# Biases as rows, a later wo and a new order on VectorE in a two-layer graph network on one core

## The chip, the cores and the metric

The kernel runs on one core of one Trainium2 chip. Its time is the device time of one execution in microseconds (us), and the figure of a version is the median of several runs. The engines are TensorE (PE in the profile, with PEld for its weight loads), VectorE (DVE), ScalarE (ACT), GpSimd (POOL) and SyncE (SP). SP, ACT and POOL also issue DMAs; in the profile, their issuing side is SPq, ACTq and POOLq.

## The reference

64 graphs of 256 nodes with 512 features each, float32, share one adjacency matrix of 0 and 1. Layer 0 is an attention of 8 heads masked by that matrix, layer 1 a product with it, and a layer norm follows each:

```python
q = (x @ Wq + bq).reshape(b, n, H, HD)          # H = 8, HD = 64
k = (x @ Wk + bk).reshape(b, n, H, HD)
v = (x @ Wv + bv).reshape(b, n, H, HD)
scores = einsum('bqhd,bkhd->bhqk', q, k) / sqrt(HD) + (1 - adj) * -1e9
out = einsum('bhqk,bkhd->bqhd', softmax(scores), v).reshape(b, n, d)
x = layernorm(x + out @ Wo + bo)
x = layernorm(x + einsum('nm,bmd->bnd', adj, x) @ weight + bias)
```

## The kernel before

**Tiling.** The graphs are taken in 32 pairs. The features of a pair lie transposed, 128 features by 512 columns (two graphs of 256 nodes), four such tiles to a pair. Each product of a pair with a 512 by 512 matrix is made in blocks of 128 output rows by 512 columns, in one PSUM bank each, by `product` (line 335 does all its matmuls). [...] a matrix is split into three parts (high, low and diff): ScalarE makes the high part, VectorE the low part and the difference, ScalarE scales one of them. So an ordinary block takes three times four matmuls. Only the first two blocks of queries and keys of pair 0 multiply unsplit float32, since nothing is split yet.

**Order.** The order on each engine is the order of the calls, written out by hand: TensorE, VectorE, ScalarE and GpSimd are under a manual schedule. `start()` is the beginning, `first(w)` and `second(w)` are one pair's steady state, `ending()` the end. `do(...)` runs its arguments one after the other. What is split in the first pairs is also written to scratch memory in DRAM by GpSimd (`keep`, line 135) and read back for each later pair (`load_w`, line 113).

**Queues.** SP issues its DMAs in the order of the code: four blocks of 128 rows of x for pair 0 (tiles `low`, line 177), columns of Wk, Wq and Wk (`load_columns`, line 172), the biases bq and bk by `by_partition` (line 90), the other halves of Wq and Wk, the adjacency, Wv (line 194) and x of pair 1 (line 81). ACT issues one, the first 128 columns of Wq. GpSimd issues four small loads of bv in `small_ones` (line 202), and the four loads of Wo in `load_o` (line 213).

**The stage of the change.** `x_first(i)` transposes block i of x on TensorE against the identity `ident` (line 262: four transposes of 128 by 128 into one bank), and VectorE (i even, line 268) or ScalarE (i odd, line 266) copies the bank to SBUF in two halves. `x_high` and `x_rest` split these tiles (lines 281, 285, 286). Then come the blocks of the first product: `(block, "q", 0, 0)`, `k 0`, `q 1`, `k 1`. ScalarE evacuates each with its bias as a column of 128 values (line 369). Between them the weights are split (`ring_high` line 121, `ring_rest` lines 126 and 127, `ring_scale` line 130), `x_t` transposes x of the next pair on VectorE (line 273), and `adj_t` transposes the adjacency on TensorE (lines 229 and 230). `scores` (line 451) and the masks (line 472) follow. `test_adj` (lines 234 to 236) checks the adjacency's values on VectorE.

The columns of biases are in `numbers`, a tile of 128 by 32: columns 0 to 3 for bq, 4 to 7 for bk, 8 to 11 for bv. bv has another order of its elements, because heads are interleaved in the transposed output; it enters only through `bv_wo` (line 242), which multiplies it with Wo, and `with_bv` (lines 249 and 250), which adds that row to bo.

Of the kernel before, what the change touches and what calls it, by code (L numbers as in the profile page):

```python
# [8 lines left out]
F32 = mybir.dt.float32  # L9
# [6 lines left out]
P = 128  # L16
# [19 lines left out]
def fast(tc, x, adj, wq, bq, wk, bk, wv, bv, wo, bo, w1, b1, out):  # L36
# [6 lines left out]
    nc = tc.nc  # L43
    B, N, D = x.shape
    HD = D // H
    DC = D // P
    NC = N // P
    NP = B // 2
    HF = D // 2
# [11 lines left out]
    one = pool("one", 1)  # L61
    two = pool("two", 2)
# [5 lines left out]
    banks = pool("banks", 8, space=bass.MemoryType.PSUM)  # L68

    XC, XF, XP, R, Q, K, V, E, SM, O, SET, HL, ST, LN = ({} for _ in range(14))  # L70
    RAW, SCRATCH, W, UNCUT, BEGUN = {}, {}, {}, {}, {}
# [14 lines left out]
            nc.sync.dma_start(t, xr[p])  # L86
            R[p] = [t[:, b] for b in range(2)]

    def by_partition(b, t):
        nc.sync.dma_start(t, b.rearrange("(c p) -> p c", p=P))  # L90

    def on_all(b, name):
        t = cpool.tile([P, D], F32, name=name)
        nc.sync.dma_start(t, b.partition_broadcast(P))
        return t
# [74 lines left out]
    def load_columns(queue, which, a, b):  # L170
        w = wq if which == "q" else wk
        queue.dma_start(RAW[which][:, :, a:b], w.rearrange("(c p) e -> p c e", p=P)[:, :, a:b])

    load_columns(nc.scalar, "q", 0, P)
    for i in range(4):
        t = four.tile([P, D], F32, name="low")
        nc.sync.dma_start(t, xc[0, i // 2, i % 2])  # L177
        rows0.append(t)
    for which, c in ("k", 0), ("q", P), ("k", P):
        load_columns(nc.sync, which, c, c + P)  # L180
    ident = one.tile([P, P], F32, name="z")
    numbers = cpool.tile([P, 32], F32, name="numbers")
    nc.scalar.activation(numbers[:, 16:17], ones[:, 0:1], AF.Exp)
    bq_s, bk_s, bv_s = (numbers[:, i * DC:(i + 1) * DC] for i in range(3))
    power, first_of_32 = numbers[:, 12:14], numbers[:, 14:15]
    by_partition(bq, bq_s)
    by_partition(bk, bk_s)
    for which in "qk":
        load_columns(nc.sync, which, HF, D)
    adj_s = two.tile([P, NC, N], F32, name="vc")  # L190
# [7 lines left out]

    def small_ones():

        for d in range(DC):
            nc.gpsimd.dma_start(bv_s[:, d:d + 1], bv.rearrange("(g h a i u) -> g a h i u", h=4, a=2, i=32, u=1)[d // 2, d % 2])
        nc.gpsimd.memset(power, -0.5)
        nc.gpsimd.memset(first_of_32, 0.0)
        for d in range(DC):
            nc.gpsimd.memset(first_of_32[d * 32:d * 32 + 1], 1.0)

    def load_o():
        for k in range(DC):
            if k % 2 == 0:  # L210
                raw_o = two.tile([P, 2, D], F32, name="hl")
            RAW["o", k] = raw_o[:, k % 2]
            nc.gpsimd.dma_start(RAW["o", k], wo[k // 2 * HF:(k // 2 + 1) * HF].rearrange("(h a i) e -> a h i e", h=4, a=2)[k % 2])

    def load_l():
        t = two.tile([P, DC, D], F32, name="r")
# [37 lines left out]
    def x_first(i):  # L254
        if i == 0:
            for h in range(2):
                XF[0, "both", h] = one.tile([P, 2, D], F32, name=f"e{2 + h}")
                for d in range(2):
                    XF[0, 2 * h + d] = XF[0, "both", h][:, d]
        pt = banks.tile([P, DC, P], F32, name="ps")  # L260
        for d in range(DC):
            nc.tensor.transpose(pt[:, d, :], rows0[i][:, d * P:(d + 1) * P], ident)  # L262
        for h in range(2):
            to, of = XF[0, "both", h][:, :, i * P:(i + 1) * P], pt[:, 2 * h:2 * h + 2]
            if i % 2:
                nc.scalar.activation(to, of, AF.Copy)
            else:
                nc.vector.tensor_copy(to, of)

    def x_t(p, k):  # L270
        if p < NP:
            XF[p, k] = two.tile([P, D], F32, name="xT")
            nc.vector.transpose(XF[p, k], XC.pop((p, k)))
            if p > 1 or k > 1:
                load_x(p + k // 2, (k + 2) % DC)
# [162 lines left out]
    def scores(p, g, between=[]):  # L438
        if not 0 <= p < NP:
            return  # L440
        for b in range(2):
            for kc in range(NC):

                sc = [banks.tile([P, 2, N], F32, name="ps") for s in range(2)]
                keys = slice(b * N + kc * P, b * N + (kc + 1) * P)
                for a in range(2):
                    digits = (1, 0, 2) if (p, g) != (0, 0) else (0,)
                    for i in digits:
                        for s in range(2):
                            r = slice(s * HD, (s + 1) * HD)  # L450
                            nc.tensor.matmul(sc[s][:, a, :], K[p, g][r, a, i, keys], Q[p, g][r, a, i, b * N:(b + 1) * N],  # L451
                                             start=i == digits[0], stop=i == digits[-1])
                if (p, g) == (NP - 1, 1):

                    names = (("x", two), ("high", four), ("low", four), ("diff", four))
                    name, pool_of = names[2 * b + kc]
                    e = [pool_of.tile([P, 2, N], F32, name=name) for _ in range(2)]
                    whole = []
                else:
                    e = one.tile([P, 2, 2, N], F32, name=f"e{2 * b + kc}")  # L460
                    whole, e = [e.rearrange("p s a n -> p (s a) n")], [e[:, s] for s in range(2)]
                E[p, g, b, kc] = e, whole
                if (b, kc) == (1, 1):
                    do(*between)
                for s in range(2):
                    nc.scalar.activation(e[s], sc[s], AF.Exp, scale=(RHO if (p, g) != (0, 0) else 1.0) * qscale)  # L466
# [15 lines left out]
    def masks(p, g, b):  # L482
        return [(masked, p, g, b, 0), (masked, p, g, b, 1), *([(summed, p, g, b)] if (p, g) != (NP - 1, 1) else [])]
# [145 lines left out]
    def do(*tasks):  # L629
        for t in tasks:  # L630
            for f, *args in (t if isinstance(t, list) else [t]):
                f(*args)
# [54 lines left out]
    def steps_of(*args):  # L687

        h, r, s = ([(f, *args, k) for k in range(4)] for f in (ring_high, ring_rest, ring_scale))
        return h[:2], r[:1] + h[2:3] + r[1:2] + h[3:], r[2:3] + s[:1] + r[3:] + s[1:2], s[2:]  # L690

    def start():
        make_identity(nc, ident)
        do(*((x_first, i) for i in range(4)), *((x_high, 0, i) for i in range(4)), (small_ones,))
        qk1, v = (steps_of(*stage) for stage in STAGES[:2])
        high, rest, scale = ([(f, "qk0", 1, k) for k in range(DC)] for f in (ring_high, ring_rest, ring_scale))
        do((block, "q", 0, 0), (x_rest, 0, 0), (x_rest, 0, 1), qk1[0], (block, "k", 0, 0), (x_rest, 0, 2), (x_rest, 0, 3), qk1[1],
           (block, "q", 0, 1), qk1[2], v[0], (block, "k", 0, 1), (x_t, 1, 0), (x_t, 1, 1), (adj_t,), qk1[3], (load_o,))
        scores(0, 0)
        do(v[1], masks(0, 0, 0), (block, "q", 0, 2), v[2], (qk_high, "q", 0, 2), (qk_rest, "q", 0, 2), v[3],  # L700
           (block, "k", 0, 2), (x_high, 1, 0), (x_high, 1, 1), (qk_high, "k", 0, 2), (qk_rest, "k", 0, 2), masks(0, 0, 1),
           (block, "q", 0, 3), (k_low, 0, 2), (qk_high, "q", 0, 3), (qk_rest, "q", 0, 3), (x_rest, 1, 0), (x_t, 1, 2),
           (block, "k", 0, 3), (stage_end, 0), (qk_high, "k", 0, 3), (qk_rest, "k", 0, 3), (x_rest, 1, 1), (x_t, 1, 3), high[:2],
           (block, "v", 0, 0), (x_high, 1, 2), high[2:], (k_low, 0, 3), (block, "v", 0, 1), (x_rest, 1, 2), (test_adj,),
           (block, "v", 0, 2), (x_high, 1, 3), (x_rest, 1, 3), (block, "v", 0, 3), (stage_end, 0), (load_r, 0), (load_l,))
        values(0, 0)
        scores(0, 1)
        do((bv_wo,), rest[:2], scale[:1], rest[2:3], scale[1:2], rest[3:], scale[2:])
        qk0 = [(f, name, 1, j) for j in range(2) for name in "qk" for f in (qk_high, qk_rest)]
        m = masks(0, 1, 0) + masks(0, 1, 1)  # L710
        do((begun, "q", 1, 0), (begun, "k", 1, 0), (block, "q", 1, 0), m[:4], qk0[:2], (block, "k", 1, 0), m[4:5], qk0[2:4], m[5:],
           (block, "q", 1, 1), (k_low, 1, 0), qk0[4:6], (o_high, 0, 0, 0), (o_high, 0, 1, 0), (o_rest, 0, 0, 0),
           (with_bv,), (block, "k", 1, 1), qk0[6:], (stage_end, 0), (k_low, 1, 1), (o_rest, 0, 1, 0))
# [242 lines left out]
```

## Time and profile before

| | us |
|---|---|
| median of 3 runs | 2396.84 (2396.31 to 2398.76) |
| the profiled execution | 2396.07 |
| its span, first to last instruction | 2394.3 |
| PE busy | 2376.7 (99%) |
| DVE busy | 1990.5 (83%) |
| ACT busy | 1502.9 (63%) |
| POOL busy | 444.6 (19%) |

A line of the timeline has the start in us from the span's beginning, the duration, the engine, the line of the kernel, the operation, the output and inputs by the program's names, how many instructions are merged, and in brackets the engine's idle time before it and what ended it. In a list of waits, the numbers are the total in us, how often, and the longest. A share of DMA over 1.00 means that packets overlap on the engines.

### The profile page before, as it was taken

Reading aid. Unit: us, or ns where it says so; the run is one execution under the profiler, and the core shown is the slowest. Engines: PE = TensorE matmul, PEld = TensorE weight load, DVE = VectorE, ACT = ScalarE, POOL = GpSimd, SP = SyncE. Lnnn points to the kernel's source line nnn. Section 1 sums busy time; section 2 is a strip of 40 time slices with the busy share of each in tenths; the row PEclk is TensorE's granted clock in tenths of the full one; section 3 lists DMA queues with packets and bytes.
Section 4 is the critical chain, followed back from the end, with each engine's and each line's share of the span. In section 5 each row is a group of like instructions: output and inputs, shape, how many; then the busy total and the mean of one; then the engine's idle time right before and its main releaser. Section 6 shows DMA issues by size and latency. Waiting matters only on the chain.

```text
span 2394.3 us, 43002 instructions
## 1 busy us (share of the span) xinstructions
PE 2376.7 (99%) x16924; PEld 1907.7 (80%) x16924; DVE 1990.5 (83%) x3310; ACT 1502.9 (63%) x2793; POOL 444.6 (19%) x759
## 2 busy tenths in 40 slices
PE   9999999999999999999999999999999999999998
PEld 6788787888878888778888788887888878878876
DVE  7989888888888888888988889888888888898867
ACT  6666566566665665656656656666566565665655
POOL 2121111121111111111111212111111111111121
PEclk9999999999999999999999999999999999999999
DMA  9987779777887777887777967778777788777782
GB/s 279 288 288 249 259 249 310 246 225 266 255 274 261 236 250 256 264 283 239 236 254 257 308 233 233 265 254 288 257 227 260 260 264 272 239 241 252 255 277 59
DMA packets 374800, 608.71 MB, mean 254 GB/s; under 512 B 273472, under 2 KB 277056, under 8 KB 314304
## 3 DMA queue, kind: packets, MB, share of 16 engines
q0 software_dynamic: 71760, 500.22, 57.2%
q1 hardware_dynamic: 302160, 105.29, 20.4%
q8 instruction: 135, 2.21, 0.4%
q14 instruction: 73, 0.60, 0.1%
q10 hardware_dynamic: 672, 0.39, 0.1%
HBM read 551.29 MB, written 49.28 MB: 251 GB/s over the span
## 4 chain that ended last, share of the span: by engine, by line
PE 99%; DMA 0%; DVE 0%; ACT 0%; SPq 0%; issue 0%; POOLq 0%; ACTq 0%
PE ps L335 74%; PE ps L417 9%; PE ps L451 8%; PE ps L611 5%; PE ps L407 3%; DMA low<-in_x_dram 0%; PE ps L561 0%; SPq L177 0%; PE ps L262 0%; ACT waste L513 0%; PE ps L242 0%; PE ps L249 0%; DVE r L563 0%; DVE r L356 0%; DVE kT L385 0%
## 5 line engine op out<-in xcount | busy, mean ns | idle before, releaser
L369 ACT ACTIVATE uncut<-ps,numbers 128x512 f32<-128x512 f32 x252 | 173.7, 689 | 274.3 <-PE ps L335 218.7
L472 DVE TENSOR_TENSOR e<-e,adjT 128x1024 f32<-128x1024 f32 x252 | 299.1, 1218 | 0.2 <-ACT e L466 0.2
L335 PE MATMUL ps<-low,wr 128*128 128x512 f32 x992 | 271.6, 395 | 0.0
L335 PE MATMUL ps<-wr,sl 128*128 128x512 f32 x1008 | 270.6, 390 | 0.1
L335 PE MATMUL ps<-wr,sh 128*128 128x512 f32 x1008 | 269.8, 389 | 0.0
L335 PE MATMUL ps<-wr,sd 128*128 128x512 f32 x1008 | 269.5, 389 | 0.0
L335 PE MATMUL ps<-high,wr 128*128 128x512 f32 x992 | 266.4, 390 | 0.0
L335 PE MATMUL ps<-diff,wr 128*128 128x512 f32 x992 | 265.0, 389 | 0.0
L519 POOL TENSOR_TENSOR ln<-ln,numbers 128x2 f32<-128x2 f32 x127 | 139.6, 1099 | 667.5 <-DVE ln L518 615.6
L466 ACT ACTIVATE e<-ps 128x512 f32<-128x512 f32 x504 | 253.0, 627 | 8.6 <-PE ps L451 8.6
L513 ACT ACTIVATE waste<-r,ln 128x512 bf16<-128x512 f32 x255 | 183.3, 719 | 104.4 <-DVE ln L506 98.5
L417 PE MATMUL ps<-e,v 128*32 128x256 f32 x4032 | 229.1, 379 | 0.0
L534 ACT ACTIVATE r<-r,ln 128x512 f32<-128x512 f32 x254 | 193.3, 809 | 55.1 <-DVE ln L524 28.0
L335 PEld LDWEIGHTS ps<-wr,sh 128*128 128x128 f32 x1008 | 189.2, 188 | 39.9
L335 PEld LDWEIGHTS ps<-wr,sd 128*128 128x128 f32 x1008 | 189.1, 188 | 39.8 <-DMA wr<-o 0.4
L335 PEld LDWEIGHTS ps<-high,wr 128*128 128x128 f32 x992 | 186.3, 188 | 41.8 <-ACT e L466 0.8
L335 PEld LDWEIGHTS ps<-diff,wr 128*128 128x128 f32 x992 | 186.2, 188 | 39.1
L335 PEld LDWEIGHTS ps<-wr,sl 128*128 128x128 f32 x1008 | 186.9, 188 | 38.2 <-issue 0.4
L381 DVE SCALAR_TENSOR_TENSOR qT<-qT,uncut 128x512 fp32r<-128x512 f32 x126 | 86.7, 688 | 147.9 <-ACT qT L374 147.8
L451 PEld LDWEIGHTS ps<-qT,kT 64*128 64x128 f32 x3056 | 187.8, 187 | 27.1 <-PE ps L417 12.3
L335 PEld LDWEIGHTS ps<-low,wr 128*128 128x128 f32 x992 | 177.6, 188 | 35.5 <-ACT wr L130 0.6
L451 PE MATMUL ps<-qT,kT 64*128 64x256 f32 x3056 | 201.7, 285 | 0.5 <-ACT kT L390 0.5
(164 smaller groups left out, 4157.0 us busy)
## 6 DMA issues: line engine op xcount, KB each, us to landing
wr<-qk POOLq DMA_DIRECT2D x183, 1024.0 KB, 7.8
wr<-v POOLq DMA_DIRECT2D x93, 1024.0 KB, 6.8
wr<-o POOLq DMA_DIRECT2D x90, 1024.0 KB, 8.2
wr<-l POOLq DMA_DIRECT2D x90, 1024.0 KB, 8.7
r<-in_x_dram SPq DMA_DIRECT2D x32, 1024.0 KB, 12.2
out_dram<-r SPq DMA_DIRECT2D x62, 512.0 KB, 2.9
x<-in_x_dram SPq DMA_DIRECT2D x488, 64.0 KB, 5.7
qk<-wr POOLq DMA_DIRECT2D x6, 1024.0 KB, 8.7
```

The lines of the kernel that those rows point to most:

```text
L335: nc.tensor.matmul(pm, *pairs[k][i], start=i == 0 and k == 0, stop=i == n - 1 and k == DC - 1)
L369: nc.scalar.activation(to, pm, AF.Identity, bias=bias[:, j:j + 1], scale=scale)
L381: nc.vector.scalar_tensor_tensor(low, high.bitcast(F32), -RHO, UNCUT.pop((name, p, j)), op0=OP.mult, op1=OP.add)
L407: nc.tensor.matmul(at[h * 32:(h + 1) * 32, b, :], ones, chunk[h], start=i == 0, stop=i == len(sm) - 1)
L417: nc.tensor.matmul(at[h * 32:(h + 1) * 32, a, :], V[p, b][:, kc, col:col + 32], E[p, g, b, kc][0][h % 2][:, h // 2, :], start=kc == 0, sto ...
L451: nc.tensor.matmul(sc[s][:, a, :], K[p, g][r, a, i, keys], Q[p, g][r, a, i, b * N:(b + 1) * N], start=i == digits[0], stop=i == digits[-1])
L466: nc.scalar.activation(e[s], sc[s], AF.Exp, scale=(RHO if (p, g) != (0, 0) else 1.0) * qscale)
L472: nc.vector.tensor_tensor(e, e, mask[:, kc:kc + 1, :].to_broadcast([P, e.shape[1], N]), op=OP.mult)
L513: nc.scalar.activation(waste, R[p][b][:, c], AF.Square, bias=t[0][:, c:c + 1], accum_out=t[1][:, c:c + 1])
L519: nc.gpsimd.tensor_tensor(t[2], t[1], power[:, cs], op=OP.pow)
L534: nc.scalar.activation(r[:, :cut], r[:, :cut], AF.Identity, scale=scale, bias=bias)
L611: nc.tensor.matmul(pm[:, j, :], t[:, i, mc, j * P:(j + 1) * P], adjT[:, mc, :], start=mc == 0 and i == 0, stop=mc == NC - 1 and i == 1)
```

## The change

There are three parts.

1. The biases bq and bk are no longer loaded by SP as columns, nor bv by GpSimd. ACT loads all three as rows into a corner of the identity's tile: 12 rows of 128 values (4 for bq, 4 for bk, 4 for bv in its own order, in two DMAs). TensorE transposes them in one go, right after the last block of x, and VectorE copies the 128 by 12 result to `numbers`.
2. `load_o` takes one block at a time, and its four DMAs on GpSimd come after the second split step of Wv, inside the second list of `start()`, in place of before `scores(0, 0)`.
3. On VectorE, the first split of Wv comes before `x_t(1, 0)` and `adj_t`, `x_t(1, 1)` after them, and `test_adj` earlier, between the blocks of queries and keys.

```diff
-    def by_partition(b, t):
-        nc.sync.dma_start(t, b.rearrange("(c p) -> p c", p=P))
...
+    room = one.tile([P, D], F32, name="z")
+    ident, rows = room[:, :P], room[:3 * DC, P:2 * P]
...
-    ident = one.tile([P, P], F32, name="z")
     numbers = cpool.tile([P, 32], F32, name="numbers")
     nc.scalar.activation(numbers[:, 16:17], ones[:, 0:1], AF.Exp)
+    for i, b in enumerate((bq, bk)):
+        nc.scalar.dma_start(rows[i * DC:(i + 1) * DC], b.rearrange("(c p) -> c p", p=P))
+    for g in range(2):
+        to = rows[2 * DC + 2 * g:2 * DC + 2 * g + 2].rearrange("a (h i) -> a h i", h=4)
+        nc.scalar.dma_start(to, bv.rearrange("(g h a i) -> g a h i", g=2, h=4, a=2)[g])
-    by_partition(bq, bq_s)
-    by_partition(bk, bk_s)
...
     def small_ones():
-        for d in range(DC):
-            nc.gpsimd.dma_start(bv_s[:, d:d + 1], bv.rearrange("(g h a i u) -> g a h i u", h=4, a=2, i=32, u=1)[d // 2, d % 2])
...
-    def load_o():
-        for k in range(DC):
-            if k % 2 == 0:
-                raw_o = two.tile([P, 2, D], F32, name="hl")
-            RAW["o", k] = raw_o[:, k % 2]
-            nc.gpsimd.dma_start(RAW["o", k], wo[k // 2 * HF:(k // 2 + 1) * HF].rearrange("(h a i) e -> a h i e", h=4, a=2)[k % 2])
+    def load_o(k):
+        if k % 2 == 0:
+            RAW["o"] = two.tile([P, 2, D], F32, name="hl")
+        RAW["o", k] = RAW["o"][:, k % 2]
+        nc.gpsimd.dma_start(RAW["o", k], wo[k // 2 * HF:(k // 2 + 1) * HF].rearrange("(h a i) e -> a h i e", h=4, a=2)[k % 2])
...
+    def biases():
+        pt = banks.tile([P, 3 * DC], F32, name="ps")
+        nc.tensor.transpose(pt, rows, ident[:3 * DC, :3 * DC])
+        nc.vector.tensor_copy(numbers[:, :3 * DC], pt)
...
-        do(*((x_first, i) for i in range(4)), *((x_high, 0, i) for i in range(4)), (small_ones,))
+        do(*((x_first, i) for i in range(4)), (biases,), *((x_high, 0, i) for i in range(4)), (small_ones,))
...
-        do((block, "q", 0, 0), (x_rest, 0, 0), (x_rest, 0, 1), qk1[0], (block, "k", 0, 0), (x_rest, 0, 2), (x_rest, 0, 3), qk1[1],
-           (block, "q", 0, 1), qk1[2], v[0], (block, "k", 0, 1), (x_t, 1, 0), (x_t, 1, 1), (adj_t,), qk1[3], (load_o,))
+        do((block, "q", 0, 0), (x_rest, 0, 0), (x_rest, 0, 1), qk1[0], (block, "k", 0, 0), (x_rest, 0, 2), (x_rest, 0, 3),
+           qk1[1], (block, "q", 0, 1), qk1[2], v[0], (block, "k", 0, 1), v[1][:1], (x_t, 1, 0),
+           (adj_t,), qk1[3])
         scores(0, 0)
-        do(v[1], masks(0, 0, 0), (block, "q", 0, 2), v[2], (qk_high, "q", 0, 2), (qk_rest, "q", 0, 2), v[3],
+        do(v[1][1:], (x_t, 1, 1), masks(0, 0, 0), (block, "q", 0, 2), v[2], *((load_o, k) for k in range(DC)), (qk_high, "q", 0, 2), (qk_rest, "q", 0, 2), v[3], (test_adj,),
...
-           (block, "v", 0, 0), (x_high, 1, 2), high[2:], (k_low, 0, 3), (block, "v", 0, 1), (x_rest, 1, 2), (test_adj,),
+           (block, "v", 0, 0), (x_high, 1, 2), high[2:], (k_low, 0, 3), (block, "v", 0, 1), (x_rest, 1, 2),
```

## The prediction

> **What bounds the kernel now.** I read the page's head first, then TensorE's own list of waits, then the timeline of the first 60 us, because the diff touches nothing later. The page:
>
> ```profile
> span 2394.3 us, 43002 instructions
> PE 2376.7 (99%) x16924; PEld 1907.7 (80%) x16924; DVE 1990.5 (83%) x3310; ACT 1502.9 (63%) x2793; POOL 444.6 (19%) x759
> ```
>
> TensorE is busy for all but 17.6 us of the span, so whatever does not move a TensorE instruction is free. Of the 17.6 us, about 11 lie behind its last matmul (it ends at 2383.1), out of the change's reach. The waits of TensorE over the whole span (in total, times, longest):
>
> ```profile
> PE ps L262 <- DMA low<-in_x_dram: 5.4, 4, 3.8
> PE ps L335 <- ACT e L266: 0.5, 1, 0.5
> PE ps L451 <- ACT kT L390: 0.5, 1, 0.5
> ```
>
> Three rows, and two of them lie in the first 10.3 us. The timeline there, and two rows further on (start, duration, instruction, idle before it and what ended it):
>
> ```profile
> 1.52 2.88 POOL L202 DMA_DIRECT2D numbers<-in_L_gnn_bv_dram  x4 [0.15 <-issue]
> 3.83 1.08 PE L262 MATMUL ps<-z,low 128*128 128x128 f32 x4 [3.83 <-DMA low<-in_x_dram]
> 4.88 1.56 SPq L90 DMA_DIRECT2D numbers<-in_L_gnn_bq_dram  x1
> 5.21 1.11 PE L262 MATMUL ps<-z,low 128*128 128x128 f32 x4 [0.29 <-DMA low<-in_x_dram]
> 6.36 0.66 ACT L266 ACTIVATE e<-ps 128x256 f32<-128x256 f32 x2 [3.62 <-PE ps L262]
> 6.48 1.90 SPq L90 DMA_DIRECT2D numbers<-in_L_gnn_bk_dram  x1
> 6.56 1.12 PE L262 MATMUL ps<-z,low 128*128 128x128 f32 x4 [0.24 <-DMA low<-in_x_dram]
> 8.71 1.12 PE L262 MATMUL ps<-z,low 128*128 128x128 f32 x4 [1.04 <-DMA low<-in_x_dram]
> 10.30 15.53 PE L335 MATMUL ps<-e,r 128*128 128x512 f32 x32 [0.47 <-ACT e L266]
> 11.08 0.69 DVE L285 SCALAR_TENSOR_TENSOR sl<-sh,e 128x512 fp32r<-128x512 f32 x1 [2.61 <-ACT sh L281]
> 26.31 0.69 DVE L230 CAST adjT<-ps 128x512 fp32r<-128x512 f32 x1 [2.10 <-PE ps L229]
> 38.68 0.69 DVE L381 SCALAR_TENSOR_TENSOR kT<-kT,uncut 128x512 fp32r<-128x512 f32 x1 [1.51 <-ACT kT L374]
> ```
>
> The four groups of transposes each wait for their rows of x; the last waits longest (1.04 us), and the first product follows it. From 10.30 to 77.7 TensorE has no idle time over 0.1 us. The same stretch by half microseconds (length, then busy time and count of PE, PEld, DVE, ACT, POOL, then clock, DMA share, GB/s) shows why the last rows are late:
>
> ```profile
> 3.50:4.00 0.50, 0.17 (x1) 0.20 (x2) 0.00 (x0) 0.00 (x0) 0.50 (x2) 1.00 1.09 399
> 4.50:5.00 0.50, 0.42 (x2) 0.01 (x1) 0.04 (x1) 0.00 (x0) 0.33 (x6) 1.00 1.48 281
> 5.00:5.50 0.50, 0.29 (x2) 0.29 (x3) 0.50 (x2) 0.00 (x0) 0.08 (x1) 1.00 0.48 58
> 5.50:6.00 0.50, 0.50 (x4) 0.42 (x2) 0.21 (x1) 0.00 (x0) 0.00 (x0) 1.00 0.28 82
> 6.50:7.00 0.50, 0.44 (x2) 0.44 (x3) 0.00 (x0) 0.50 (x2) 0.00 (x0) 1.00 0.89 235
> ```
>
> Between 5 and 6 us the DMA engines move 70 KB where they moved 190 KB per half microsecond before. In these very microseconds GpSimd's single-element loads of bv move their first packets (queue 0 shows its first packets in 4 to 5) and SP issues the single-element load of bq.
>
> [...] weight loads of the first product come every 0.86 us until 13.03 and every 0.43 us from 13.66.
>
> **Part 1, biases as rows.** *Removed:* from SP, 1.56 + 1.90 = 3.46 us of issue; from GpSimd, 2.88 us and 512 single elements. GpSimd's next work is a copy at 21.03, so only the DMA engines feel it. *Gain:* by 4.5 us the windows sum to 0.89 MB of the 1.31 MB that the four x loads (1.05) and the first block of Wq (0.26) need. At the 380 GB/s of 3.0 to 4.5 us the remaining 0.42 MB take 1.1 us, so the last packet would go at 5.6 us, and landing some 0.8 us later gives 6.4 in place of 8.67. TensorE can't use all of that: the second group ends at 6.32, the third could run 6.32 to 7.44, the fourth 7.44 to 8.56 in place of 9.83. So the gain is at most 1.27 us (0.24 + 1.04) and at least nothing, if the dip has another cause. I take 0.95: the fourth group starting near 7.75.
>
> *Added on ACT's queue:* four issues. Nearest row: ACT's own issue of Wq, 0.46 us each. [...] the two bv rows wait for Wq's first block (0.75 + 3.8 = 4.55) and the first x rows (3.80). So 2.74 to 3.66 for bq and bk, 4.55 to 5.47 for bv. Behind them on ACT stands the copy at 6.36: 0.9 us of cover, and it idles 3.62 us there now. If an issue cost what bq's did (1.56), that copy would be 1.3 us late and with it the transposes' PSUM copies; I take nothing. *Landing:* from 3.0 us (the fastest x load) to 7.0 (bq as columns) after the last issue at 5.0, so 8.0 to 12.0. I take 3.5: [...] 8.5.
>
> *Added on TensorE:* one transpose of 12 rows, behind the fourth group and ahead of the first product. Four full ones take 1.12, so 0.28 at most. It fits into the 0.47 us in which TensorE waits for ACT's copy; without that cover, 0.28. *Added on VectorE:* one 128x12 copy, between 0.07 (the 128x16 fill) and 0.28 (the 128x16 scale at 52.24), inside its 2.61 us wait before 11.08. Nothing. One more PSUM bank in turn: all eight are free that early.
>
> *SP's order:* the two loads of Wq and Wk columns 128 to 256 now wait for the second and third x rows (5.2 and 6.5) in place of issuing at 3.08 and 3.66. They are read at 17.2 and 20.6; even at 7.8 us to landing they are there by 14.5. Everything behind (wq and wk halves, adjacency, wv, x of the next pair) comes up to 1 us sooner; no TensorE wait after 10.3 is for a DMA, so nothing.
>
> **Part 2, wo later.** Four issues (0.68 each) move behind two copies of v's parts, from 28.41 to about 37. Behind them in turn: one copy of v and, at 46.96, GpSimd's next load. wo takes 14.0 us to land now; 37 + 14 to 40 + 14 gives 51 to 54, read at 59.38 less the gain. 4 us of cover; past it TensorE pays one for one.
>
> **Part 3, VectorE's order.** Per piece: the first wv split pair (2 x 0.69) goes ahead of the copy of the transposed adjacency, where VectorE now waits 2.10 us; one 0.65 transpose goes behind. So the masks behind (29.57) start within 0.1 us of before. The adjacency test (0.07 + 0.69 + 0.08 + 0.28 = 1.12) goes from 51.4 into the 1.51 us gap before 38.68. The stretch it leaves ends in a wait for ACT's PSUM copy (0.84 before 57.09), so the 0.47 us wait at 77.7 stays. Nothing, and every row after these is in the same order on each engine.
>
> **Sum.** -0.95 on 2396.07, the profiled execution (span 2394.3 and 1.8 around it), is 2395.1. The median stands 0.77 above it; from 2396.84 it gives 2395.9. About 0.2%, 4.8 us, is what a measurement can tell from no change; this is a fifth of it.
>
> **Rivals.**
> *Bias rows land late (slower).* TensorE stands before its transpose, and every product behind it. For: bq took 7.0 us, and the rows go last. [...] It decides from a landing at about 9.95 (10.30 - 0.28, less semaphore time): at 12.0 the first product starts near 12.35, 2.05 late: 2398.9.
> *The dip has another cause,* [...] the last x rows still land at 8.67: 2396.8.
> *The clock.* Denser transposes may release the clock one window sooner: 3.1 us of half-speed product become 1.6: 1.5 less on top, 2394.4. [...]
> *wo late,* behind 2 MB of copies that share its queue: if it landed at 64 us, TensorE would stand some 5: 2401.8. Against: queue 0 moves 3.1 MB between 44 and 52.
>
> **How the numbers follow.** Main case 0.58 (own range 2395.3 to 2396.5); dip stays 0.16; rows late 0.14; clock 0.07; wo or another new wait 0.05. The range 2394.3 to 2398.2 leaves out half of the late rows, the wo case and a little of the clock. Faster by over 0.2% would need 4.8 us; all idle time between 3.83 and 78.2 is 2.5 and the half clock 1.6, so 0.03 for what the trace doesn't show. Slower by over 0.2%: 0.03, out of wo and new waits.
>
> **What would show it.** Right: no dip at 5 to 6 us, fourth transposes before 8.3, first product at 9.1 to 9.6, the 12-row transpose without a wait over 0.2. Wrong: a wait of that transpose on the rows; x still landing near 8.7; ACT's first copy after 6.4; a wait before the bv and wo product; any new row in TensorE's waits.

## The result and the profile after

| | before | after |
|---|---|---|
| median of 13 runs, us | 2396.17 (2393.87 to 2398.76) | 2391.58 (2391.06 to 2393.82) |
| the profiled execution, us | 2396.07 | 2391.06 |
| its span, us | 2394.3 | 2389.2 |

The ratio of the times is 0.9982, with an interval from 0.9973 to 0.999. The change gains 4.6 us, 0.19%: a real gain, just inside the 0.2% named as the bound, and below the predicted range of 2394.3 to 2398.2.

The two spans differ by 5.1 us. Three places hold nearly all of it: the first product starts sooner, it runs at full clock from its beginning, and the time behind TensorE's last matmul is shorter. From the head of the page of the kernel after:

```profile
PE 2374.3 (99%) x16925; PEld 1907.5 (80%) x16925; DVE 1991.0 (83%) x3311; ACT 1505.4 (63%) x2793; POOL 443.5 (19%) x755
```

TensorE is busy 2.4 us less, with one instruction more. That is the first hint that a clock is concerned, since no matmul was taken away. Its list of waits, after (total, times, longest):

```profile
PE ps L261 <- DMA low<-in_x_dram: 4.1, 2, 3.8
PE ps L455 <- ACT kT L394: 0.5, 1, 0.5
PE ps L271 <- issue: 0.2, 1, 0.2
```

Waits for x went from four with 5.4 us to two with 4.1 us. That is 1.3 us, not 5. The timeline of the start, after:

```profile
1.32 0.58 ACTq L184 DMA_DIRECT2D z<-in_L_gnn_bq_dram  x1
3.77 1.09 PE L261 MATMUL ps<-z,low 128*128 128x128 f32 x4 [3.77 <-DMA low<-in_x_dram]
4.49 0.57 ACTq L187 DMA_DIRECT2D z<-in_L_gnn_bv_dram  x2
5.16 2.54 PE L261 MATMUL ps<-z,low 128*128 128x128 f32 x12 [0.30 <-DMA low<-in_x_dram]
7.89 0.20 PE L271 MATMUL ps<-z 12*128 12x12 f32 x1 [0.19 <-issue]
8.13 0.17 DVE L272 COPY numbers<-ps 128x12 f32<-128x12 f32 x1 [0.21 <-PE ps L271]
8.18 14.00 PE L339 MATMUL ps<-e,r 128*128 128x512 f32 x32
```

Twelve transposes stand in one row of 2.54 us: groups two, three and four no longer wait between one another. The first product starts at 8.18 in place of 10.30. The dip of the DMA engines at 5 to 6 us is gone (columns as in the windows of the prediction; last is GB/s):

```profile
5.00:5.50 0.50, 0.34 (x2) 0.34 (x3) 0.50 (x2) 0.00 (x0) 0.00 (x0) 1.00 1.00 365
5.50:6.00 0.50, 0.50 (x4) 0.49 (x3) 0.16 (x1) 0.00 (x0) 0.00 (x0) 1.00 1.06 357
```

They move 361 KB in that microsecond, where the kernel before moved 70. Now the weight loads of the first product (PEld), after:

```profile
8.71 0.19 PEld L339 LDWEIGHTS ps<-e,r 128*128 128x128 f32 x1 [0.24 <-issue]
9.14 0.19 PEld L339 LDWEIGHTS ps<-e,r 128*128 128x128 f32 x1 [0.24 <-issue]
```

They come every 0.43 us from the start. Before, they came every 0.86 us until 13.03. In the trace's records of the granted clock, full clock begins at 7.28 us in place of 13.42. The clock column of the windows reads 1.00 already at 4 us, and so does not show this first release; the spacing of the loads does.

At the transposes of the adjacency, the first work behind the four first blocks, the gain is 3.66 us: 2.12 from the earlier start and 1.54 from the clock. First the kernel before, then after:

```profile
25.67 0.60 PE L229 MATMUL ps<-z,vc 128*128 128x128 f32 x4
```

```profile
22.01 0.60 PE L228 MATMUL ps<-z,vc 128*128 128x128 f32 x4
```

From there to beyond 2000 us the two traces keep their distance. The last matmuls, first of the kernel before, then after:

```profile
2382.90 0.22 PE L774 MATMUL ps<-numbers,ones 128*32 128x1 f32 x2
```

```profile
2379.01 0.22 PE L779 MATMUL ps<-numbers,ones 128*32 128x1 f32 x2
```

From their ends (2383.12 and 2379.23) to the ends of the spans it is 11.18 us before and 9.96 after: 1.2 us more gained where no instruction of the program was changed. Only the trace's records, and no view of them, show what shrank: GpSimd's closing drain, 7.70 us before and 6.48 after. So the sum is 3.66 + 1.2, and 0.2 from a step between the two profiles near 2098 us, which the change does not explain: 5.1. These are the parts in one execution of each kernel; the one of the kernel after is the fastest of its 13, and the repeat below has smaller parts at the start.

### The profile page after: what moved, and what is told of

Read it like the earlier page. It is cut to its first block, busy times and chain, and to the rows that moved or that the text cites. A ratio compares the mean times of both kernels' runs of the same rounds, so it can differ in the third digit from the quotient of the medians.

```text
span 2389.2 us, 43002 instructions
## 1 busy us (share of the span) xinstructions
PE 2374.3 (99%) x16925; PEld 1907.5 (80%) x16925; DVE 1991.0 (83%) x3311; ACT 1505.4 (63%) x2793; POOL 443.5 (19%) x755
## 4 chain that ended last, share of the span: by engine, by line
PE 96%; DVE 1%; ACT 0%; issue 0%; POOLq 0%; ACTq 0%
PE ps L339 72%; PE ps L421 9%; PE ps L455 8%; PE ps L615 5%; PE ps L411 3%; DVE e L476 0%; DVE wr L124 0%; DVE wr L123 0%; PE ps L565 0%; DVE kT L389 0%; DVE qT L387 0%; DVE qT L385 0%; ACT kT L394 0%; DVE kT L385 0%; ACT waste L517 0%
```

## The experiments

The kernels ran in four series; each series has its own runs of the kernel before (medians 2395.66, 2395.48, 2395.41, 2395.75), and differences below are against those. "First product" and "clock" are when the first product starts and when the trace records full clock, in the profiled execution of the run.

**Which part?** Part 1 alone keeps the loads of Wo and the order of VectorE as before:

```diff
-    by_partition(bq, bq_s)
-    by_partition(bk, bk_s)
+    for i, b in enumerate((bq, bk)):
+        nc.scalar.dma_start(rows[i * DC:(i + 1) * DC], b.rearrange("(c p) -> c p", p=P))
...
+        do(*((x_first, i) for i in range(4)), (biases,), *((x_high, 0, i) for i in range(4)), (small_ones,))
```

> Part 1 alone (biases as rows on ACT's queue), wo and VectorE's order as before. If the whole gain comes out of the first 10 us: first product at 8.0 to 8.5 us, the last block of x landed by 6.8, and 4 to 5 us less than before, as with all three parts. If wo or VectorE's order matter: less than 3.7 us of gain, with a new wait of TensorE between 22 and 80 us.

The kernel before with parts 2 and 3 alone:

```diff
-           (block, "q", 0, 1), qk1[2], v[0], (block, "k", 0, 1), (x_t, 1, 0), (x_t, 1, 1), (adj_t,), qk1[3], (load_o,))
+           qk1[1], (block, "q", 0, 1), qk1[2], v[0], (block, "k", 0, 1), v[1][:1], (x_t, 1, 0),
+           (adj_t,), qk1[3])
...
```

> Parts 2 and 3 alone (wo later, VectorE's order), biases loaded as before. If the gain is all in the first 10 us: first product at 10.3 us as before, within 1 us of the time before. If these parts matter: 1 us or more faster, seen as TensorE's matmuls catching up after 25 us.

Measured: part 1 alone 2392.65 (ratio 0.9987, 0.9981 to 0.9994), 3.0 us less than before; parts 2 and 3 alone 2395.47 (0.9998, 0.9989 to 1.0006), no difference. Part 1 alone has first product 8.15, clock 7.21 and a tail behind the last matmul of 9.95 us: the early gain and the short tail are both part 1's. But its profiled execution took 2394.17, and waits of TensorE appear in it that neither kernel has (the one for kT is in both, at 0.5 us). From the list for part 1 alone:

```profile
PE ps L340 <- ACT wr L127: 1.1, 2, 0.6
PE ps L456 <- ACT kT L395: 0.8, 1, 0.8
PE ps L422 <- ACT v L365: 0.7, 1, 0.7
PE ps L412 <- DVE sm L485: 0.3, 1, 0.3
```

All of these lie between 50 and 78 us. Farther up, VectorE stands 6.15 us before a transpose of x of the next pair (timeline, part 1 alone):

```profile
26.41 0.71 DVE L278 STREAM_TRANSPOSE xT<-x 128x512 f32<-128x512 f32 x1 [6.15 <-DMA x<-in_x_dram]
```

So parts 2 and 3 show no gain by themselves but are perhaps worth something beside part 1. The last group of runs below comes back to it.

**Whose is the dip?** In the kernel before, only the four loads of bv moved, from the first list to the front of `load_o`; then only bq and bk moved, behind the other halves of Wq and Wk:

```diff
     def small_ones():
-        for d in range(DC):
-            nc.gpsimd.dma_start(bv_s[:, d:d + 1], ...)
...
     def load_o():
+        for d in range(DC):
+            nc.gpsimd.dma_start(bv_s[:, d:d + 1], ...)
```

> Before, with only GpSimd's four single-element loads of bv moved from 1.5 us to the front of the loads of wo (28 us). If they cause the dip of the DMA engines at 5 to 6 us: no dip, the last block of x lands at 6.5 to 7.5 in place of 8.7, first product at 8.2 to 9.2. If SP's loads of bq and bk, or the crowd of weight loads, cause it: dip stays, last block of x at 8.4 or later, first product at 10 or later.

```diff
-    by_partition(bq, bq_s)
-    by_partition(bk, bk_s)
     for which in "qk":
         load_columns(nc.sync, which, HF, D)
+    by_partition(bq, bq_s)
+    by_partition(bk, bk_s)
```

> Before, with only SP's single-element loads of bq and bk moved behind the second halves of Wq and Wk; bv stays at 1.5 us. If bv causes the dip: dip stays, last block of x at 8.4 or later, first product at 10 or later. If SP's single-element loads cause it: last block of x at 6.5 to 7.5, first product at 8.2 to 9.2. If each has a share: between.

With bv late: 2393.35 (0.999, 0.9982 to 0.9998), 2.3 us less. With bq and bk late: 2395.58 (1.0, 0.9991 to 1.0008). The windows at 5 us, first with bv late, then with parts 2 and 3 alone, which leave bv where it was:

```profile
5.00:5.50 0.50, 0.28 (x2) 0.28 (x3) 0.50 (x2) 0.00 (x0) 0.00 (x0) 1.00 0.99 270
5.50:6.00 0.50, 0.50 (x4) 0.50 (x4) 0.23 (x1) 0.00 (x0) 0.00 (x0) 1.00 1.04 377
```

```profile
5.00:5.50 0.50, 0.28 (x2) 0.28 (x3) 0.50 (x2) 0.00 (x0) 0.09 (x1) 1.00 0.98 109
5.50:6.00 0.50, 0.50 (x4) 0.44 (x3) 0.23 (x1) 0.00 (x0) 0.00 (x0) 1.00 0.29 86
```

The dip is there with bv's loads and gone without them; with bv late, the last rows of x land at 6.62 and the first product starts at 8.51. One profile does not settle it, as the other run shows: with bq and bk late, three of 13 executions took 2392.55 to 2393.38 and the other ten 2395.3 to 2397.2. The profiled one is the fastest of the three, and has no dip (295 and 275 GB/s) though bv is loaded in it. The medians then say, since the time falls with bv late and not with bq and bk late, that bv's single elements make the dip in most executions, not in all; and the loads of bq and bk, which took SP 3.46 us to issue, cost nothing that the medians show.

Is it the single elements, or that GpSimd issues them? The kernel after, with the two row loads of bv issued by GpSimd in place of ACT:

```diff
-        nc.scalar.dma_start(to, bv.rearrange("(g h a i) -> g a h i", g=2, h=4, a=2)[g])
+        nc.gpsimd.dma_start(to, bv.rearrange("(g h a i) -> g a h i", g=2, h=4, a=2)[g])
```

> The changed kernel, with the two row loads of bv issued by GpSimd at 0.8 us in place of ACT. If the single elements cause the dip at 5 to 6 us: no dip, first product at 8.0 to 8.7 as in the change. If any load of GpSimd in that stretch causes it: dip, first product at 9.8 or later. The end: if GpSimd's closing drain grows with its elements, 10.0 us from TensorE's last matmul to the end as in the change; if it grows with the number of its loads, 10.3 to 10.6; if with any small load, 11.2.

2391.71 (0.9984, 0.9978 to 0.9991), 3.7 us less than before, as the change itself has it below. There is no dip (364 and 351 GB/s), and the tail is 10.11 us. So loads of GpSimd at that time do not make the dip by themselves: bv's single elements do. Whether they would make it from another queue was not tried. In all profiles with columns of single elements the tail was 11.18 to 11.20, bv late or not; in all with rows issued by ACT 9.95 to 9.97. Whether the columns of bv or those of bq and bk lengthen GpSimd's drain was not told apart.

**The clock.** The kernel before, with transposes of the identity put between those of x, so that TensorE does not rest there:

```diff
+    def warm(n):
+        pt = banks.tile([P, P], F32, name="ps")
+        for _ in range(n):
+            nc.tensor.transpose(pt, ident, ident)
...
-        do(*((x_first, i) for i in range(4)), ...
+        do((warm, 8), (x_first, 0), (warm, 1), (x_first, 1), (warm, 1), (x_first, 2), (warm, 4), (x_first, 3), ...
```

> Before, with extra transposes of the identity on TensorE (8 ahead of the first block of x, 1, 1 and 4 between the blocks), so that TensorE works without a gap from 1.4 us on. x still lands at 8.7 us in most executions. If the half clock costs 1.5 us because the gaps keep the window from filling: weight loads of the first product 0.43 us apart from its first one, 1.0 to 1.8 us faster than before. If the clock is a matter of chance or transposes don't count as work: still 0.86 apart for about 3 us, within 0.5 us of before.

The change once more, beside it:

> The changed kernel once more, beside the others of this set: 4 to 5 us faster than before; first product at 8.0 to 8.3 us.

The change: 2391.75 (0.9984, 0.9977 to 0.9991), 3.7 us less than before, short of the 4 to 5 expected. In its profile the first product starts at 8.68, 1.62 us sooner than before and not 2.12, full clock comes at 9.37, and the adjacency at 22.84, a gain of 2.83 and not 3.66. So a part of what the first profile shows was luck. The kernel before with its transposes filled up: 2394.28 (0.9997, 0.9989 to 1.0005), a median 1.2 us lower, with an interval that includes no change. Its profiled execution shows the mechanism apart from the dip: the last rows of x still land late (8.39), the first product starts at 10.01, but at full clock:

```profile
10.01 5.42 PE L340 MATMUL ps<-e,r 128*128 128x512 f32 x12 [0.47 <-ACT e L266]
23.85 0.60 PE L229 MATMUL ps<-z,vc 128*128 128x128 f32 x4
```

The adjacency follows 13.84 us behind it where the kernel before takes 15.37. That is the 1.53 us of the clock.

When does the clock come? In the one profile below that records three changes at its start (both parts as before, on eleven transposes), they lie at 4.17, 28.07 and 31.48: the first two seven times 3.41 us apart, the last two once. In the profiles of the kernel before and after, the clock falls to half behind the last matmul, at 2385.69 and 2382.96, which is 695 and 696 times 3.413 us behind the release. So stretches of 3.41 us, counted back from the release in each profile, are taken as its windows here; that the clock is decided by how busy they are is the author's reading of the figures that follow. In the kernel before, TensorE was busy 64% of 6.60 to 10.01 (1.08 + 1.12 us of transposes) and was not released at its end; it was released at 13.42, after a window busy to 91%, from 10.30 on. In the kernel after it was busy 91% of 3.87 to 7.28 (0.99 + 2.12), and was released. In this last window only transposes ran (the trace lists them as MATMUL), so here they count as work for the clock.

How full the window must be does not come out to the per cent. In the starts of all profiles, no window busy to 76% or less brought full clock, and every one busy to 88% or more did. Between them it went both ways: with bv late, 3.65 to 7.06 (86%) brought none and the next window, also 86%, did; of the versions below, the one with eleven transposes and both parts as before was released after a window busy to 80% (0.76 to 4.17), the one with eight in front was not after one to 79% (1.87 to 5.28). Where the edge of the window falls differs from run to run: the other profiles of the change and of its neighbours have releases at 7.21, 8.84, 9.37, 10.37 and 10.71.

**More of it on top of the change.** Eight transposes ahead of x, and the biases transposed only behind the first block of queries, where they can't hold it up:

```diff
-        do(*((x_first, i) for i in range(4)), (biases,), *((x_high, 0, i) for i in range(4)), (small_ones,))
+        do((warm, 8), *((x_first, i) for i in range(4)), *((x_high, 0, i) for i in range(4)), (small_ones,))
...
-        do((block, "q", 0, 0), (x_rest, 0, 0), (x_rest, 0, 1), qk1[0], ...
+        do((begun, "q", 0, 0), (x_rest, 0, 0), (x_rest, 0, 1), (biases,), (block, "q", 0, 0), qk1[0], ...
```

> The changed kernel, with 8 extra transposes of the identity ahead of x, and the transpose of the bias rows behind the first block of queries, so that it can't hold the first product up. If the clock is then full before the x transposes end: they take 0.6 us a block in place of 0.85, first product at 7.7 to 8.0 us, 0.2 to 0.5 us faster than the change. If x rows set it: first product at 8.0, no change.

The same, with the first columns of Wq asked for behind ACT's first ACTIVATE. In the source that is still ahead of the biases; in the trace ACT issues the biases from 0.75 us on and Wq behind them, at 3.45:

```diff
-    load_columns(nc.scalar, "q", 0, P)
...
     nc.scalar.activation(numbers[:, 16:17], ones[:, 0:1], AF.Exp)
+    load_columns(nc.scalar, "q", 0, P)
```

> As the run with extra transposes and the rows later, and the first columns of Wq loaded behind the bias rows on ACT's queue, so that x has the DMA engines alone. If the DMA engines' share sets x: last block of x lands at 5.9 in place of 6.55, first product at 7.2 to 7.6 us, 0.6 to 1.0 us faster than the change, unless VectorE's work then ends later than TensorE wants it (new waits at 50 to 80 us, and nothing gained). If Wq becomes the last to land: first product at 8 us or later.

Neither gains. The first took 2391.93, the same as the change (2391.75): its eight transposes end at 3.40, two gaps of 0.34 and 0.36 us remain before the second group of x, and the clock came at 8.69, behind the start of the first product at 8.51. The second took 2393.48: the third group of x waits 1.06 us, and the columns of Wq land at 8.96, last of all, so that the first product waits 0.62 us for them and starts at 9.10; the clock comes at 12.74.

With eleven in front and one behind the first group, both gaps close:

```diff
-        do((warm, 8), *((x_first, i) for i in range(4)), ...
+        do((warm, 11), (x_first, 0), (warm, 1), *((x_first, i) for i in range(1, 4)), ...
```

> The changed kernel, with 11 extra transposes ahead of the first block of x and one behind it, rows transposed behind the first block of queries. If a window has to be filled by about nine tenths: clock full before 8.2 us in every execution and before 7 in most, first product at 7.6 to 8.2 and at full clock, 0.3 to 0.8 us faster than the change. If x's landing sets it all: no faster than the change.

The timeline with eleven:

```profile
1.43 2.61 PE L277 MATMUL ps<-z 128*128 128x128 f32 x11 [1.43 <-POOL z masks.py:199]
3.83 1.06 PE L261 MATMUL ps<-z,low 128*128 128x128 f32 x4
4.69 0.42 PE L277 MATMUL ps<-z 128*128 128x128 f32 x1
5.24 2.03 PE L261 MATMUL ps<-z,low 128*128 128x128 f32 x12
7.73 3.27 PE L344 MATMUL ps<-e,r 128*128 128x512 f32 x7 [0.47 <-ACT e L265]
```

2390.97 (0.9984, 0.9977 to 0.999), 4.4 us less than before. In the same series the change with bv's rows on GpSimd took 2391.71, so this is 0.74 us faster (0.4 to 1.2 when the runs of both are resampled). Full clock comes at 6.14, the twelve transposes of x take 2.03 us in place of 2.54, and all 21 runs lie within 1.3 us. The change itself was not run in this series; its medians in two others were 2391.58 and 2391.75. That this version beats the change too is likely, but the two were not measured side by side.

**What parts 2 and 3 do beside part 1.** Parts 1 and 2, then parts 1 and 3. Each is the change with one part as before: VectorE's order, or Wo asked for ahead of `scores(0, 0)`:

```diff
-           qk1[1], (block, "q", 0, 1), qk1[2], v[0], (block, "k", 0, 1), v[1][:1], (x_t, 1, 0),
-           (adj_t,), qk1[3])
+           (block, "q", 0, 1), qk1[2], v[0], (block, "k", 0, 1), (x_t, 1, 0), (x_t, 1, 1), (adj_t,), qk1[3])
         scores(0, 0)
-        do(v[1][1:], (x_t, 1, 1), masks(0, 0, 0), ...
+        do(v[1], masks(0, 0, 0), ...
```

> Parts 1 and 2 (bias rows, wo later), VectorE's order as before. If VectorE's order is what closes the waits that part 1 alone has between 50 and 78 us: they stay (0.5 us or more in all beyond the 0.47 at the end of that stretch), about 1 us slower than the change. If the place of wo closes them: no such waits, as fast as the change.

```diff
-           (adj_t,), qk1[3])
+           (adj_t,), qk1[3], [(load_o, k) for k in range(DC)])
         scores(0, 0)
-        do(... v[2], *((load_o, k) for k in range(DC)), (qk_high, "q", 0, 2), ...
+        do(... v[2], (qk_high, "q", 0, 2), ...
```

> Parts 1 and 3 (bias rows, VectorE's order), wo as early as before. If VectorE's order closes the waits: none between 50 and 75 us, within 0.5 us of the change. If the place of wo does: the waits of part 1 alone, about 1 us slower than the change.

2391.74 (3.7 us less than before) and 2392.46 (3.0 less); resampled, the difference of the two is from -0.2 to 1.8 us, so not shown. Because the chance of the clock (full at 7.21 to 10.71 in the profiles of the change and its neighbours) may hide such amounts, the same three undoings were made once more on the version with eleven transposes, whose runs agree more closely: that version again, with Wo early, with VectorE's order before, and with both before. Their diffs are the two above, made on it, alone and together.

> The kernel with eleven extra transposes once more, as the base of this set: 2390.6 to 2391.9, no wait of TensorE over 0.2 us between 8 and 74 us.

> The base with wo asked for early, before the first scores, as before the change. If early wo delays x of the next pair, for which VectorE's order then no longer matters: x transposes on VectorE wait for their load, new waits of TensorE between 50 and 75 us, 0.7 to 1.5 us slower than the base. If only VectorE's order counts: as the base.

> The base with VectorE's order as before the change, wo late. If VectorE's order counts (both x transposes ahead of the adjacency, the adjacency test late): new waits of TensorE between 50 and 75 us, 0.7 to 1.5 us slower than the base. If only the place of wo counts: as the base.

> The base with both as before the change, that is bias rows and the extra transposes alone: 0.7 to 2 us slower than the base, waits as in the run of the bias rows alone. If one of the two is enough to avoid the waits, it is slower than both runs with one of them.

| eleven transposes, and | median, us | runs | over 2392 |
|---|---|---|---|
| nothing else | 2391.01 | 21 | 2 |
| Wo early | 2391.47 | 16 | 6 |
| VectorE's order before | 2391.33 | 20 | 2 |
| both before | 2392.63 | 13 | 7 |

Both together cost 1.6 us in the median (0.15 to 4.1 resampled), and they cost it in some executions only. Alone, Wo early costs 0.5 us (-0.1 to 1.8, so not shown, though six of its 16 runs are over 2392) and VectorE's order before 0.3 (0.1 to 0.5). Whether one of the two parts would do is not shown either: both before against either one alone has an interval that includes nothing. The profiled execution with both before took 2395.28. Its timeline shows a wait that the kernel after doesn't have:

```profile
26.57 0.71 DVE L282 STREAM_TRANSPOSE xT<-x 128x512 f32<-128x512 f32 x1 [5.56 <-DMA x<-in_x_dram]
27.20 0.65 DVE L229 CAST adjT<-ps 128x512 fp32r<-128x512 f32 x1
27.91 1.96 PE L460 MATMUL ps<-qT,kT 64*128 64x256 f32 x6 [1.89 <-DVE adjT L229]
29.80 1.95 PE L344 MATMUL ps<-sl,wr 128*128 128x512 f32 x4
```

VectorE waits 5.56 us for x of the next pair. Behind that transpose, in its order, stands the copy of the adjacency out of PSUM, and TensorE waits 1.89 us for that copy. The last line shows a second price: four matmuls take 1.95 us, where the same four take 1.20 in the version with nothing undone. Windows of the same execution, at and after the wait (clock third from the right):

```profile
27.50:28.00 0.50, 0.09 (x2) 0.09 (x2) 0.50 (x2) 0.00 (x0) 0.15 (x1) 1.00 1.09 434
28.00:28.50 0.50, 0.50 (x4) 0.42 (x5) 0.47 (x2) 0.00 (x0) 0.00 (x0) 0.57 1.00 377
```

The clock is at half from 28.07 to 31.48, one window of 3.41 us. By the product of bv and Wo this execution is 4.47 us behind (60.08 against 55.61): 0.30 of it from the start, 1.89 from the wait, and 2.28 behind it, of which half clock can account for at most 1.7 (half of 3.41). With part 1 alone, the copy of the adjacency starts as late (27.04) without a wait of TensorE for it; what it costs differs from version to version. What makes x of the next pair late is argued, not tested: it is issued behind much else, and Wo and the copies to scratch memory load the DMA engines at the same time.

## Why the prediction was wrong

It put the gain at 0.95 us; the measured one is 4.6. Its sum had one term, the earlier start, and mis-sized it; two more were left out of it, the clock and the end of the program. In the two profiles the three measure 2.12, 1.54 and 1.2.

- **The dip and its cause: right.** It is gone at 5 to 6 us, and bv's single elements made it (with bv late, 2.3 us less). That SP's load of bq has a share in it was not borne out.
- **"The gain is at most 1.27 us (0.24 + 1.04)": wrong, 2.12.** The cap added up waits and took 1.12 us as the length of a group of four transposes: "the third could run 6.32 to 7.44, the fourth 7.44 to 8.56". 1.12 is one group alone. In a row the groups start 0.85 us apart, and 2.54 us holds three, the last of them partly at full clock. What ended at 9.83 ends at 7.70, not 8.56. The value of 0.95 inside that cap was then too careful as well: x landed at 6.55, near the 6.4 that the sum of bytes gave.
- **The clock at 7%: wrong.** The size was right: 1.5 predicted, 1.54 measured, with some luck (1.21 in the repeat: 2.83 - 1.62). The chance was not: it was held to be a separate stroke of luck, by the author's estimate. It follows from the main case: with x on time the transposes close up (twelve in 2.54 us), and TensorE was busy 91% of the window before the release at 7.28, with transposes alone. Some of the half-clock time is saved in every profile of the change, whole or with part 2 or 3 undone: between first product and full clock lie at most 1.63 us (8.74 to 10.37, with VectorE's order before) against 3.12 in the kernel before. So the two terms should have been added, in the likeliest case too.
- **"About 11 lie behind its last matmul, out of the change's reach": wrong, 1.2.** GpSimd's drain at the end took 7.70 us with the columns loaded at the start and 6.48 with the rows. The bound that put a gain of 4.8 us out of reach (2.5 of idle time and 1.6 of half clock) lacked this term.
- **ACT's queue, the landing of the rows, the 12-row transpose, VectorE's copy: right in what they cost.** ACT issued bq at 1.32, not at 2.74 as the author had estimated, the rows landed at 7.8 (8.5 was the author's estimate), the transpose took 0.20 after a wait of 0.19 and stayed within the old gap of 0.47, the copy took 0.17. The rival of late rows and that of a late Wo did not come.
- **Parts 2 and 3, "nothing": right alone, wrong beside part 1.** Each was priced against the kernel before, where TensorE comes to the adjacency at 25.67 and x of the next pair is there by then. With part 1 TensorE comes up to 3.7 us sooner, and with both parts undone, on the version with eleven transposes, some executions lose time (seven of 13 over 2392); in the one profiled, the copy behind the transposes of x is late. The wait is shown for that execution, its share in the others is argued. "No TensorE wait after 10.3 is for a DMA, so nothing" read the kernel before rightly, but says nothing of one 3.7 us ahead of it, in which VectorE waits for x (6.15 us with part 1 alone, 5.56 with eleven transposes) and TensorE can come to wait for VectorE.

## What to carry to other kernels

When a start gets shorter, price the next limit too: how long the work takes without gaps (spacing of starts, not the length of a lone group), what the denser work does to the clock, and what the rest now arrives too early for. Load small vectors as rows and turn them on TensorE, since here the profile with columns of single elements moved 70 KB from 5 to 6 us in place of 361, and its end was 1.2 us longer. If TensorE idles before its data come, transposes of the identity can bring full clock before the first product: eleven, with one more to close the gap behind the first rows, did in every profile (4.17 to 6.14); eight, with gaps of 0.34 and 0.36 us, left the time as it was (2391.93 against 2391.75).

## What was unexpected of the hardware

- Transposes alone brought full clock here: at 7.28, and at 5.66 and 6.14 with eleven in front, before any other matmul had run. No window at the start busy to 76% or less ended in full clock, every one from 88% on did, and at 79 to 86% it went both ways.
- In one execution, half clock came back for 3.41 us around a single wait of 1.89 us: it began at 28.07, behind a window with 55% of its time idle (24.65 to 28.07), while one with 27% idle in the same execution (4.17 to 7.59) did not bring it.
- The end of the program was 1.2 us longer in every profile with columns of single elements (11.18 to 11.20, against 9.95 to 9.97 with rows on ACT and 10.11 with bv's rows on GpSimd), even though they were loaded more than 2300 us earlier.
- ACT issued DMAs at 1.32 us, while its load of the function table (1.25 to 2.53) was still running.
